# A four-way selective scan: another assignment of states to engines, and other costs for the planner that orders the scan pass

## Chip, cores and metric

The kernel runs on one core of one Trainium2 chip. The metric is the device time of one execution in microseconds, as the median of several runs. The core has five engines with instruction queues of their own: TensorE (PE; its weight loads are listed apart as PEld), VectorE (DVE), ScalarE (ACT), GpSimd (POOL) and SyncE (SP), which here only issues transfers.

## What is computed

Eight images of 64 x 64 positions with 96 channels go through a state-space layer and then through attention and a feed-forward layer. Nearly all of the time is in the selective scan of the first layer: 192 inner channels, 4 directions, 16 states, 4096 positions.

```
def _selective_scan(u, delta, A, Bs, Cs, D):
    def step(h, inps):
        d_t, u_t, b_t, c_t = inps
        h = h * jnp.exp(d_t[..., None] * A) + (d_t * u_t)[..., None] * b_t[:, :, None, :]
        y = jnp.einsum('bkdn,bkn->bkd', h, c_t)
        return (h, y)
    h0 = jnp.zeros(u.shape[:3] + (A.shape[-1],), u.dtype)
    _, ys = jax.lax.scan(step, h0, (dT, uT, BT, CT))
    y = jnp.moveaxis(ys, 0, -1)
    return y + D[None, :, :, None] * u
```

For each channel and each state n: a decay exp(delta·A), an input delta·u·B, a recurrence over the positions, and a sum over the states weighted by C. Group norm, projections, a 3 x 3 convolution and SiLU come before it; layer norm, gating, linear attention (no softmax) and a quantized feed-forward layer after it.

## The kernel before

`pass1` makes the scan's inputs, `pass2` is the scan, `pass3` the rest. Only `pass2` is concerned here.

**Chunks.** `pass2` works in 192 chunks (`pieces`, line 544) of 128 partitions by T = 1024 positions. A pair of images gives three kinds, c = 0, 1, 2. Kinds 0 and 1 hold the first 128 channels of one image each. Kind 2 holds the last 64 channels of both images ("two-batch chunk", `chunk_rows`, line 68). Each kind has 4 directions k with 4 chunks each, so it takes 16 chunks in a row. There are 128 chunks of kinds 0 and 1, and 64 of kind 2; the pass is a sequence of twelve sections of 16 chunks.

**One state of one chunk.** ACT makes the decay `da` (`decay`). The input times B, `dbu`, is made in PSUM, in a tile `wide`, in one of three ways, which `WAYS` (line 55) assigns by state, one pair of lists for kinds 0 and 1 and one for kind 2:

- by ACT (first list, `scaled`, line 651): ACT multiplies the transposed input `duT` by a column of B, in eight instructions of 128 x 128, or sixteen of 128 x 64 in a two-batch chunk, into a tile `x`; PE transposes it back into `wide` in eight instructions;
- by POOL (second list, `scaled_by_pool`, line 666): the same in one instruction of 128 x 1024, or two of 128 x 512, into `xg`; PE transposes it as before;
- by DVE (all other states, `products`, lines 691 to 699): PE spreads B over the partitions with two matmuls into `wide`, and DVE multiplies by `du`.

Then DVE runs the recurrence, `scan`, one TENSOR_TENSOR_SCAN per state. For each two states POOL multiplies by C (`times_c`, TENSOR_TENSOR c<-c,h) and PE adds the terms in `acc` (`sum_over_n`).

**Preparation.** While a chunk runs, `prepare` (line 561) makes the inputs of the next. It takes three `wide` tiles as well: for B transposed (PE wide<-sel,xb; ACT copies it to `bT`), for delta (PE wide<-xdt,dt_w; ACT computes the softplus, between two loads of its function tables) and for the transposed input (PE wide<-ident,du; ACT copies it to `duT`). POOL makes `du` from delta in between.

**Buffers.** Tiles come from rings (`room`, line 538): 3 `wide`, 3 `x`, 3 `da`, 3 `h`, 6 `c`, one `xg`. The n-th `wide` tile in the order of taking uses the buffer of the (n-3)-th, so whoever fills it first on PE waits until that one was read for the last time: by its scan on DVE, or by ACT's copy where it was a tile of the preparation.

**Order.** The order of the instructions on each engine is fixed when the program is built. Each step is a generator that yields the engine that it needs and a cost in us; `weave` (line 142) keeps a clock for each engine and always takes the step that can begin first, with a rank for ties, so the costs decide what stands ahead of what. `InOrder` (line 83) keeps every engine to that order. On the chip an engine works its queue in order: an instruction that has to wait holds up what stands behind it.

Of the kernel before, what the change touches and what calls it, by code (L numbers as in the profile page):

```python
# [51 lines left out]
NPC = L // T  # L52
NT = T // P

WAYS = [([2, 4, 6, 8, 10, 12, 14, 15], [3, 9]), ([3, 5, 7, 10, 13, 15], [2, 6, 12])]
NS = 3

LATE = 5
# [9 lines left out]
def chunk_rows(pair, c):  # L68

    b0 = 2 * pair  # L70
    if c < 2:
        return [(slice(0, P), b0 + c, slice(0, P))]
    return [(slice(64 * j, 64 * j + 64), b0 + j, slice(P, DI)) for j in range(2)]
# [456 lines left out]
def pass2(ctx, tc, g, ident, engines, fixed, u_d, xd_d, b_d, dt_d, y_d):  # L530
# [3 lines left out]
    pe, dve, act, pool = engines  # L534
# [4 lines left out]
    slots = {name: Slots(count) for name, count in room.items()}  # L539
# [9 lines left out]
    def take(name, shape, dtype=F32):  # L549

        return pools[name].tile(shape, dtype, name=name), slots[name].taken
# [6 lines left out]
    def spread(n, c):  # L558
        return sel[:, c, n : n + 1].to_broadcast([KB, P]) if c < 2 else sel2[:, n, :]
# [91 lines left out]
    def scaled(at, n):  # L651

        pair, c, _, _ = pieces[at]
        yield "duT", at
        x, (_, _, _, _, duT, bT) = None, made[at]
        for i in range(0, NT, 2):
            end = yield ("act", 0.6, 0.2) if i else ("act", 0.6, 0.2, slots["x"])
            if i == 0:
                x, slot = take("x", [P, NT, P])
            for i2 in (i, i + 1):  # L660
                for j, (part, _, _) in enumerate(chunk_rows(pair, c)):
                    act.mul(x[:, i2, part], duT[:, i2, part], bT[:, i2, j * N + n : j * N + n + 1])
        made["x", at, n] = x, "x", slot
        done["x", at, n] = end

    def scaled_by_pool(at, n):
        pair, c, _, _ = pieces[at]
        yield "duT", at
        end = yield "pool", 2.5, 0.2, slots["xg"]
        x, slot = take("xg", [P, NT, P])  # L670
        _, _, _, _, duT, bT = made[at]
        for j, (part, _, _) in enumerate(chunk_rows(pair, c)):
            wide = part.stop - part.start
            b = bT[:, :, j * N + n : j * N + n + 1].to_broadcast([P, NT, wide])
            pool.tensor_mul(x[:, :, part], duT[:, :, part], b)
        made["x", at, n] = x, "xg", slot
        done["x", at, n] = end

    def products(at, n):

        pair, c, _, _ = pieces[at]
        by_act, by_pool = WAYS[c // 2]
        if n in by_act or n in by_pool:
            yield "x", at, n
            end = yield "pe", 1.3, 0.2, slots["wide"]
            dbu, slot = take("wide", [P, T])
            x, name, of_x = made["x", at, n]
            for i in range(NT):
                pe.transpose(dbu[:, i * P : (i + 1) * P], x[:, i, :], ident)
            slots[name].release(of_x, end)  # L690
        else:
            yield "du", at
            end = yield "pe", 0.7, 0.2, slots["wide"]
            dbu, slot = take("wide", [P, T])
            xb = made[at][0]
            for q in range(0, T, GRP):
                pe.matmul(dbu[:, q : q + GRP], spread(n, c), xb[:, q : q + GRP], start=True, stop=True)
            end = yield "dve", 1.28, 0.0
            dve.tensor_mul(dbu, made[at][3], dbu)
        made["dbu", at, n] = dbu, slot  # L700
        done["dbu", at, n] = end
# [122 lines left out]
    for at, (pair, c, k, pc) in enumerate(pieces):  # L824
        by_act, by_pool = WAYS[c // 2]

        def add(kind, lead, unit, n=0):
            units.append((kind, at * N + n - lead, unit))

        add("prep", 8, prepare(at))  # L830
        for n in range(N):
            if n % 2 == 0:
                add("c", 12, load_c(at, n // 2), n)
            add("da", 2, decay(at, n), n)
            if n in by_act:
                add("x", 5, scaled(at, n), n)
            elif n in by_pool:
                add("xg", 4, scaled_by_pool(at, n), n)
            add("dbu", 1, products(at, n), n)
            add("scan", 0, scan(at, n), n)  # L840
            if n % 2 == 1:
                if at % NPC < NPC - 1:
                    add("carry", -2, carries(at, n // 2), n)
                add("term", 0, times_c(at, n // 2), n)
                add("sum", -4, sum_over_n(at, n // 2), n)
        add("acc", 0, take_acc(at), N)
# [289 lines left out]
```

## Time and profile before

| | |
|---|---|
| median of 3 runs | 10446.42 us (10441.61 to 10449.34) |
| the profiled execution | 10448.65 us, span 10446.9 us |
| scan pass, first to last recurrence | 758.9 to 9545.1 us of the span |
| one section of kinds 0 or 1 (16 chunks) | about 720 us |
| one section of kind 2 (16 chunks) | about 757 us |
| granted TensorE clock, mean | 0.896 |

A row of the costliest groups gives an engine, an operation, its result and operands with their shapes, the count, the busy time in us, the mean duration of one in ns, and the idle time of the engine just before. Busy time counts overlapping instructions once, so busy time divided by the count is less than the mean duration where instructions overlap. The table by windows gives for each stretch of time its length and then, for each engine, busy time and the number of instructions in brackets. The list of waits gives who waited for whom, the sum in us, how often, and the longest. In the timeline, equal instructions in a row are one line: start, length, engine, instruction, count, and in square brackets the idle time ahead of it and the releaser. All instructions carry line 91, a helper's line, and are told apart by the names of their tiles.

### The profile page before, as it was taken

To read this page: it belongs to the slowest core of one execution; us is meant where nothing else is said; L and a number is where in the kernel's file an instruction comes from. 1 tells how busy PE (TensorE), PEld (TensorE's weight loads), DVE (VectorE), ACT (ScalarE), POOL (GpSimd) and SP (SyncE) were. 2 spreads that over 40 slices of the span, in tenths; PEclk is the share of its full clock that TensorE was granted. 3 is DMA by queue.
4 is the path that set the end of the run, shared out by engine and by line. 5 is a ranking of instruction groups with operands and counts; after the bars stand their busy time and mean duration, and the time that the engine had idled before them with its cause. 6 is when DMAs were issued, how large, how long until landed. Compare 5 with 4: busy or idle time off the path is not lost.

```text
span 10446.9 us, 154273 instructions
## 1 busy us (share of the span) xinstructions
PE 7673.1 (73%) x52768; PEld 6378.4 (61%) x52768; DVE 9496.8 (91%) x6822; ACT 9405.8 (90%) x21523; POOL 9212.9 (88%) x3271
## 2 busy tenths in 40 slices
PE   6757777777777777777777777777777777776887
PEld 3326666666666666666666666666666666665775
DVE  6869999999999999999999999999999999997786
ACT  5759999999999999999999999999999999996665
POOL 1539999999999999999999999999999999997886
PEclk8879999998899999988999999989999999887776
DMA  5766676688976666788866666899666667897442
GB/s 153 234 189 218 220 237 211 220 206 198 206 216 211 214 221 201 219 201 198 220 213 214 217 209 215 203 200 209 219 206 218 217 203 220 200 199 181 128 131 61
DMA packets 928018, 2103.39 MB, mean 201 GB/s; under 512 B 274391, under 2 KB 422648, under 8 KB 925700
## 3 DMA queue, kind: packets, MB, share of 16 engines
q1 hardware_dynamic: 919812, 2092.79, 70.5%
q8 instruction: 422, 6.91, 0.3%
q14 instruction: 360, 2.95, 0.1%
q10 hardware_dynamic: 7424, 0.74, 0.1%
HBM read 1917.59 MB, written 175.66 MB: 200 GB/s over the span
## 4 chain that ended last, share of the span: by engine, by line
ACT 43%; DVE 17%; PE 15%; issue 14%; POOL 7%; DMA 4%; SPq 1%; ACTq 0%; DVEq 0%; POOLq 0%
ACT x L91 19%; ACT da L91 16%; DVE h L91 12%; PE acc L91 6%; PE wide L91 4%; POOL c L91 3%; DVE wide L91 3%; ACT L91 2%; PE mm L91 2%; ACT y L91 1%; ACT delta L91 1%; DMA xd_d<-xd 1%; ACT duT L91 1%; PE px L91 1%; PE pa L91 1%
## 5 line engine op out<-in xcount | busy, mean ns | idle before, releaser
L91 POOL TENSOR_TENSOR c<-c,h 128x2048 f32<-128x2048 f32 x1536 | 6964.2, 4551 | 260.9 <-DVE h L91 135.1
L91 DVE TENSOR_TENSOR_SCAN h<-da,carry,wide 128x1024 f32<-128x1024 f32 x2304 | 5262.1, 2331 | 283.0 <-PE wide L91 196.3
L91 ACT ACTIVATE x<-duT,bT 128x128 f32<-128x128 f32 (+1 forms) x14336 | 4188.5, 367 | 65.2 <-PE wide L91 60.9
L91 PE MATMUL acc<-ident,c 128*128 128x128 f32 x24576 | 3451.6, 296 | 653.8 <-POOL c L91 648.8
L91 PEld LDWEIGHTS acc<-ident,c 128*128 128x128 f32 x24576 | 3120.0, 154 | 982.8 <-POOL c L91 834.2
L91 ACT ACTIVATE da<-delta,a_neg 128x1024 f32<-128x1024 f32 x3072 | 3502.6, 1143 | 213.3 <-DVE h L91 201.6
L91 PE MATMUL wide<-ident,x 128*128 128x128 f32 x11264 | 1573.2, 287 | 661.1 <-DVE h L91 634.6
L91 PEld LDWEIGHTS wide<-ident,x 128*128 128x128 f32 x11264 | 1326.8, 147 | 926.3 <-issue 388.5
L91 DVE TENSOR_TENSOR_SCAN h<-da,wide 128x1024 f32<-128x1024 f32 x768 | 1709.6, 2271 | 114.7 <-PE wide L91 80.6
L91 DVE TENSOR_TENSOR wide<-du,wide 128x1024 f32<-128x1024 f32 x1216 | 1463.6, 1209 | 115.1 <-PE wide L91 115.0
L91 PE MATMUL wide<-xb,sel 96*128 96x512 bf16 x2432 | 760.8, 397 | 575.0 <-DVE h L91 470.1
L91 POOL TENSOR_TENSOR xg<-duT,bT 128x512 f32<-128x512 f32 (+1 forms) x640 | 892.0, 1409 | 107.7 <-PE wide L91 94.8
L91 PEld LDWEIGHTS <-sel 96*128 96x128 bf16 x2432 | 217.1, 100 | 725.3 <-DVE h L91 462.6
L91 POOL TENSOR_TENSOR du<-delta,u 128x1024 f32<-128x1024 f32 x192 | 455.0, 2370 | 200.2 <-ACT delta L91 91.1
L91 PE MATMUL wide<-ident,xg 128*128 128x128 f32 x3584 | 520.8, 293 | 131.0 <-DVE h L91 128.2
L91 PEld LDWEIGHTS wide<-ident,xg 128*128 128x128 f32 x3584 | 448.0, 153 | 175.3 <-issue 84.3
L91 ACT ACT_TABLE_LOAD x385 | 494.0, 1283 | 7.1
L91 DVE SCALAR_TENSOR_TENSOR u<-xpad,conv_w,u 128x4096 f32<-128x4096 f32 x96 | 456.2, 4752 | 1.9
L91 PE MATMUL px<-u,w_xp 128*128 128x512 f32 x512 | 256.8, 642 | 80.0 <-ACT u L91 47.9
L91 PE MATMUL wide<-ident,du 128*128 128x128 f32 x1536 | 213.8, 284 | 106.3 <-DVE h L91 77.9
L91 PE MATMUL mm<-w_out,gt 128*128 128x96 f32 (+1 forms) x1024 | 260.6, 374 | 34.6 <-POOL gt L91 16.4
L91 PEld LDWEIGHTS wide<-ident,du 128*128 128x128 f32 x1536 | 176.3, 146 | 137.7 <-issue 86.4
(133 smaller groups left out, 6271.4 us busy)
## 6 DMA issues: line engine op xcount, KB each, us to landing
c<-xd_d SPq DMA_DIRECT2D x1024, 1024.0 KB
c<-xd_d SPq DMA_DIRECT2D x1024, 512.0 KB
u<-u_d SPq DMA_DIRECT2D x128, 512.0 KB
xdt<-dt_d SPq DMA_DIRECT2D x1152, 36.0 KB
xb<-b_d SPq DMA_DIRECT2D x384, 96.0 KB
u<-u_d SPq DMA_DIRECT2D x128, 256.0 KB
y_d<-y SPq DMA_DIRECT2D x24, 1024.0 KB
y<-y_d SPq DMA_DIRECT2D x64, 384.0 KB
```

The source lines that it names most:

```text
L91: ins = getattr(self.engine, op)(*args, **kwargs).ins
```

## The change

Two things change, both inside `pass2`. The lists of states in `WAYS` are others. In kinds 0 and 1 the number of states for each engine stays at 8 for ACT, 2 for POOL and 6 for DVE. In kind 2 it goes from 6, 3 and 7 to 5, 3 and 8. And three of the costs that the planner reckons with are others: a quarter of an ACT product in a two-batch chunk 1.0 instead of 0.6 us, a POOL product 2.0 us (2.2 in a two-batch chunk) instead of 2.5 us, and a DVE product 1.22 instead of 1.28 us. The costs are used only when the program is built.

```diff
-WAYS = [([2, 4, 6, 8, 10, 12, 14, 15], [3, 9]), ([3, 5, 7, 10, 13, 15], [2, 6, 12])]
+WAYS = [([2, 5, 6, 8, 11, 12, 14, 15], [3, 7]), ([2, 3, 7, 9, 14], [0, 5, 12])]
...
         for i in range(0, NT, 2):
-            end = yield ("act", 0.6, 0.2) if i else ("act", 0.6, 0.2, slots["x"])
+            cost = 0.6 if c < 2 else 1.0
+            end = yield ("act", cost, 0.2) if i else ("act", cost, 0.2, slots["x"])
...
         yield "duT", at
-        end = yield "pool", 2.5, 0.2, slots["xg"]
+        end = yield "pool", 2.0 if c < 2 else 2.2, 0.2, slots["xg"]
         x, slot = take("xg", [P, NT, P])
...
-            end = yield "dve", 1.28, 0.0
+            end = yield "dve", 1.22, 0.0
             dve.tensor_mul(dbu, made[at][3], dbu)
```

## The prediction

> **What bounds the kernel now.** The page's first lines show three engines near full.
>
> ```profile
> PE 7673.1 (73%) x52768; PEld 6378.4 (61%) x52768; DVE 9496.8 (91%) x6822; ACT 9405.8 (90%) x21523; POOL 9212.9 (88%) x3271
> ```
>
> The average mixes stages, so I read the table by windows next: one section of kind 1, one of kind 2, then the first two directions (four chunks each) of the former. After the length come PE, PEld, DVE, ACT, POOL, then clock, DMA share and GB/s.
>
> ```profile
> 3679.90:4400.10 720.20, 527.43 (x3969) 460.07 (x3969) 684.85 (x353) 684.53 (x1491) 676.52 (x178) 0.93 0.66 214
> 4400.10:5157.30 757.20, 552.22 (x3889) 474.02 (x3888) 706.65 (x370) 744.12 (x1982) 713.06 (x240) 0.89 0.91 204
> 3679.90:3855.30 175.40, 130.62 (x989) 112.96 (x988) 170.55 (x89) 168.92 (x360) 167.53 (x44) 0.94 0.68 222
> 3855.30:4038.10 182.80, 129.09 (x948) 111.55 (x949) 172.18 (x89) 174.26 (x382) 170.38 (x46) 0.92 0.63 208
> ```
>
> Kind 2 is bound by ACT: 744.1 of 757.2 us, idle 13.1; DVE idles 50.6. Kinds 0 and 1 have no full engine: DVE and ACT idle 35 of 720 us each. In the list of waits, DVE's idle time there has one cause:
>
> ```profile
> DVE h L91 <- PE wide L91: 27.0, 14, 3.8
> DVE wide L91 <- PE wide L91: 2.8, 3, 1.5
> ```
>
> Fourteen waits in 16 chunks: about once a chunk. One of them in the timelines, DVE first, then PE:
>
> ```profile
> 3918.35 4.58 DVE L91 TENSOR_TENSOR_SCAN h<-da,carry,wide 128x1024 f32<-128x1024 f32 x2
> 3924.90 2.35 DVE L91 TENSOR_TENSOR_SCAN h<-da,carry,wide 128x1024 f32<-128x1024 f32 x1 [1.97 <-PE wide L91]
> ```
>
> ```profile
> 3915.03 1.07 PE L91 MATMUL wide<-ident,x 128*128 128x128 f32 x8 [1.72 <-DVE h L91]
> 3915.93 1.91 PE L91 MATMUL acc<-ident,c 128*128 128x128 f32 x16
> 3917.68 0.35 PE L91 MATMUL wide<-sel,xb 96*128 96x16 bf16 x8
> 3919.58 1.09 PE L91 MATMUL acc<-ident,c 128*128 128x128 f32 x8 [1.55 <-POOL c L91]
> 3920.75 0.75 PE L91 MATMUL wide<-xdt,dt_w 108*128 108x512 bf16 x2
> 3921.29 1.92 PE L91 MATMUL acc<-ident,c 128*128 128x128 f32 x8
> ```
>
> The x product is state 8. Two preparation tiles follow, B (sel,xb) and delta (xdt,dt_w), then state 9. With three `wide` buffers state 9 reuses state 8's, and PE cannot begin it before scan 8 ends (3922.9). DVE has nothing between scans 8 and 9, so it stands for the transposes' time. In the built order B and delta stand like this, with no product between, in 164 of 192 chunks. Matched with DVE's timeline: in kinds 0 and 1 the 105 such chunks wait 1.95 us ahead of state 9 and take 45.22 us; the 23 where a product stands between wait 0.06 and take 44.12. In the table above three of the first direction's four chunks are of the second sort, none of the second direction's.
>
> **What the skill says.** PSUM — Partial Sum Buffer, "Engine vs sequencer instructions": matmuls start and complete in program order, and the other engines' queues are strict FIFO. The PE rows agree. Perfetto Trace Analysis, "Optimization Strategy": the same gap repeating on an engine that should be saturated can mean too little SBUF or PSUM for the next tile; the gap at state 9 is one. ScalarE: Activation LUTs, "What ACT_TABLE_LOAD costs": an ACTIVATE with a pointer operand takes some 280 + 0.833·N ns and overlaps the next by 93 ns; for N = 64, 333 less 93 is 240. The trace has 336 and, by busy time over count, 254; I use 254.
>
> **The change part by part.** The rows for the prices:
>
> ```profile
> L91 ACT ACTIVATE x<-duT,bT 128x64 f32<-128x64 f32 x6144 | 1558.5, 336 | 7.3 <-PE wide L91 5.0
> L91 DVE TENSOR_TENSOR wide<-du,wide 128x1024 f32<-128x1024 f32 x1216 | 1463.6, 1209 | 115.1 <-PE wide L91 115.0
> ```
>
> (a) One state of each of 64 two-batch chunks leaves ACT for DVE. ACT loses 64 x 16 x 1558.5/6144 = 260 us, 65 a section: 744 becomes 679. DVE gains 64 x 1463.6/1216 = 77 us, 19.2 a section: 706.6 becomes 725.8. PE loses 8 transposes a chunk (1573.2/11264 = 0.140 each) and gains two matmuls (760.8/2432 = 0.313): less by 0.5 us, which costs nothing, as PE has 205 idle us in the section. The bound passes from ACT to DVE, with POOL (713) close behind.
>
> (b) The states moved between lists in kinds 0 and 1, and POOL's 2, 6, 12 to 0, 5, 12, change no count. Durations are the same, so they act only through the order, (c).
>
> (c) The new costs add and remove nothing; they move instructions. In the changed kernel's built order B and delta are adjacent in 5 chunks instead of 164: state 9 or 8 now stands between them. So the wait at state 9 goes from 159 chunks. What is late next: delta now waits for scan 8 instead of 7, and the copy to `duT` stands one state closer to its need. ACT still reaches softplus just after decay 11, one state before the product that takes delta's buffer, as before (decay 10, state 11). Every transfer stays, on SP; POOL's xg of state 7 stands six scans ahead of use (state 9's stood ten), enough at 2.6 us each. DMA in kind 2 is busy 0.91 x 757 = 687 us; in a shorter section this hides still, though it would be the next limit.
>
> What is left idle I take from the trace: the first direction above, mostly in the new pattern, leaves DVE 4.85 us in four chunks, 19.4 a section. Kinds 0 and 1: the eight sections took 5762.6 us with DVE busy 5479.9; 5479.9 + 8 x 19.4 = 5635, less by 127. (The comparison by chunks gives 105 x 1.10 = 116.) Kind 2: 3023.6 us in four sections, DVE busy 2823.1; plus 77 and 4 x 19.4 makes 2978, less by 46. Sum: 173 off the profiled execution's 10448.65, or 10275; the median stands 2.2 below, so **10273 us**.
>
> The residual idle is the one term that no row shows for the new order. Low end: the limiting engine idles only ACT's 13.1 us of today's kind 2. Then 5479.9 + 8 x 13.1 and 2900.1 + 4 x 13.1 give 249 less, 10198. High end: the next paragraph.
>
> **Rivals.** *Half given back.* ACT (684.5) and POOL (676.5) are as loaded as DVE in kinds 0 and 1, and a queue in order passes on any lateness. Only half of 127 arrives, and kind 2, now with DVE at 726 and POOL at 713, stands still: 10446 - 64 = 10382. For it: 0.7 us waits at state 7 already show in the 23 chunks. Against it: ACT reaches 98% in kind 2 today with the same queues.
>
> *A late first state in two-batch chunks* (slower). State 0 now goes through POOL: du, duT's copy on ACT, xg (2.1 us), PE (1.1), then the scan. Decay 15 stands ahead of the copy and needs scan 12's buffer; from there 1.05 + 1.0 + 2.1 + 1.1 = 5.3 us stand against three scans and two multiplications, 9.3. If a c term (4.55) comes between, 0.6 is missing; a second one makes it 5.1 a chunk. That is 64 x 5.1 = 326 on top, and without the gain in kind 2 the sum is -127 + 326: 10645. It decides against the change from 2.7 us a chunk (173/64). Against it: one c term stands there in the order, and starts after scan 11.
>
> *DVE idles as before.* If the stall only changes place, 35 and 50 us a section stay and (a) adds 77: 10523. Against it: the 23 chunks.
>
> *Nothing moves.* Excluded by the built order.
>
> **Chances.** Forecast 0.65 (10190 to 10345), half given back 0.22 (10345 to 10430), the two slower cases together 0.09, no visible change 0.04. The range, 10190 to 10400, holds the first and most of the second. About 0.2% (21 us) is what a measurement here can tell from no change. Faster 0.87, same 0.04, slower 0.09.
>
> **What would show it.** Right: windows of kinds 0 and 1 near 704 us with DVE busy still 685; of kind 2 near 745 with DVE 726 and ACT 679; DVE's wait for PE wide near 10 us a section instead of 30. Wrong: sections of 720 with the same wait at another state, or waits of DVE for a PE wide that waits for POOL xg at state 0.

## The result

The changed kernel takes 10286.21 us (median of 4 runs, 10274.94 to 10288.48), the kernel before 10447.88 (4 runs): a ratio of 0.9843, 95% interval 0.9826 to 0.986, or 162 us less. The forecast was 10273. The profiled execution of the changed kernel took 10274.94 us with a span of 10273.2, its fastest run; its span is 173.7 shorter than before.

From the page of the changed kernel, busy time, share of the span and instructions of each engine:

```profile
PE 7658.3 (75%) x52384; PEld 6303.1 (61%) x52384; DVE 9587.1 (93%) x6886; ACT 9155.6 (89%) x20499; POOL 9206.3 (90%) x3271
```

ACT has lost 250 us and DVE has gained 90. The table by windows, the sections of kind 1 and kind 2 that answer to those shown of before:

```profile
3617.30:4318.60 701.30, 533.44 (x3974) 457.03 (x3973) 685.78 (x352) 677.33 (x1481) 676.16 (x178) 0.93 0.69 220
4318.60:5060.60 742.00, 541.62 (x3785) 458.12 (x3784) 726.54 (x386) 694.72 (x1740) 712.75 (x239) 0.90 0.93 208
```

Kind 1 went from 720.2 to 701.3 us with DVE as busy as before: what went is idle time, 35 us down to 15.5. Kind 2 went from 757.2 to 742.0, and its fullest engine is now DVE (726.5), no longer ACT (694.7). Who DVE waited for in that section of kind 1 (sum, times, longest):

```profile
DVE h L91 <- PE wide L91: 4.0, 3, 2.7
DVE wide L91 <- PE wide L91: 1.4, 2, 0.7
```

Before, it was 27.0 and 2.8. The same place of a chunk as in the prediction, in the timelines of the changed kernel, PE first, then DVE:

```profile
4032.19 0.35 PE L91 MATMUL wide<-sel,xb 96*128 96x16 bf16 x8
4032.93 0.59 PE L91 MATMUL wide<-xb,sel 96*128 96x512 bf16 x2 [0.39 <-DVE h L91]
4034.90 1.45 PE L91 MATMUL acc<-ident,c 128*128 128x128 f32 x8 [1.38 <-POOL c L91]
4036.14 1.06 PE L91 MATMUL wide<-xdt,dt_w 108*128 108x512 bf16 x2
4036.99 1.06 PE L91 MATMUL wide<-xb,sel 96*128 96x512 bf16 x2
```

```profile
4028.32 6.80 DVE L91 TENSOR_TENSOR_SCAN h<-da,carry,wide 128x1024 f32<-128x1024 f32 x3
4035.03 1.21 DVE L91 TENSOR_TENSOR wide<-du,wide 128x1024 f32<-128x1024 f32 x1
4036.34 2.35 DVE L91 TENSOR_TENSOR_SCAN h<-da,carry,wide 128x1024 f32<-128x1024 f32 x1
4038.61 1.21 DVE L91 TENSOR_TENSOR wide<-du,wide 128x1024 f32<-128x1024 f32 x1
```

Product 9 (wide<-xb,sel at 4032.93) now stands between B's tile (sel,xb) and delta's (xdt,dt_w). PE fills it while DVE still runs the three scans that end with state 8, delta's tile waits in its place, and product 10 is ready before scan 9 ends. DVE's rows have no bracket: it did not stop. The two groups that priced the moved state, kept apart by shape:

```profile
L91 ACT ACTIVATE x<-duT,bT 128x64 f32<-128x64 f32 x5120 | 1315.5, 335 | 1.8
L91 DVE TENSOR_TENSOR wide<-du,wide 128x1024 f32<-128x1024 f32 x1280 | 1544.2, 1208 | 56.6 <-PE wide L91 54.9 <-ACT x L91 1.4 <-issue 0.2
```

1558.5 - 1315.5 = 243 us less on ACT (260 expected) and 1544.2 - 1463.6 = 81 more on DVE (77 expected).

### The profile page after: what moved, and what is told of

Read it like the earlier page. It is cut to its first block, busy times and chain, and to the rows that moved or that the text cites. A ratio compares the mean times of both kernels' runs of the same rounds, so it can differ in the third digit from the quotient of the medians.

```text
span 10273.2 us, 152438 instructions
## 1 busy us (share of the span) xinstructions
PE 7658.3 (75%) x52384; PEld 6303.1 (61%) x52384; DVE 9587.1 (93%) x6886; ACT 9155.6 (89%) x20499; POOL 9206.3 (90%) x3271
## 4 chain that ended last, share of the span: by engine, by line
ACT 29%; DVE 28%; issue 15%; PE 14%; POOL 10%; DMA 4%; SPq 1%; DVEq 0%; ACTq 0%; POOLq 0%
DVE h L91 20%; ACT x L91 11%; ACT da L91 11%; POOL c L91 7%; PE acc L91 6%; DVE wide L91 5%; PE wide L91 3%; ACT L91 2%; PE mm L91 2%; ACT y L91 1%; DVE u L91 1%; ACT delta L91 1%; POOL xg L91 1%; DMA xd_d<-xd 1%; DMA c<-xd_d 1%
## 5 line engine op out<-in xcount | busy, mean ns | idle before, releaser
L91 ACT ACTIVATE x<-duT,bT 128x128 f32<-128x128 f32 (+1 forms) x13312 | 3969.7, 368 | 1.9
L91 PEld LDWEIGHTS wide<-ident,x 128*128 128x128 f32 x10752 | 1304.4, 150 | 851.0 <-ACT x L91 393.0
L91 DVE TENSOR_TENSOR wide<-du,wide 128x1024 f32<-128x1024 f32 x1280 | 1544.2, 1208 | 56.6 <-PE wide L91 54.9
L91 PE MATMUL wide<-xb,sel 96*128 96x512 bf16 x2560 | 818.8, 403 | 692.6 <-DVE h L91 685.1
L91 PE MATMUL wide<-ident,xg 128*128 128x128 f32 x3584 | 483.2, 279 | 114.4 <-DVE h L91 112.6
L91 PEld LDWEIGHTS wide<-ident,xg 128*128 128x128 f32 x3584 | 411.5, 144 | 145.3 <-issue 111.7
L91 ACT COPY y<-acc 128x1024 f32<-128x1024 f32 x192 | 192.5, 1002 | 87.1 <-PE acc L91 86.7
L91 PEld LDWEIGHTS mm<-w_out,gt 128*128 128x128 f32 (+1 forms) x1024 | 202.0, 243 | 101.0 <-issue 34.6
```

Source lines behind the costliest of these rows:

```text
L91: ins = getattr(self.engine, op)(*args, **kwargs).ins
```

## The experiments

Two questions were open. The first is whether the neighbourhood of B's and delta's tiles was the cause in kinds 0 and 1. The second is what the costs and the lists do apart. All runs below were compared with the kernel before on the same chip (there 10460 us). The row "before" of the table, and its waits and lines below, come from the first chip, where it took 10448. The table gives the mean length of a section, from the first recurrence of one to that of the next, over the eight sections of kinds 0 and 1 and the four of kind 2, and in how many of the 128 and 64 chunks the two tiles are adjacent in the built order (the preparation ahead of the first chunk is counted with kinds 0 and 1). Waits ahead of one state are summed over DVE's timeline, those of more than 0.3 us.

| run | lists | costs | adjacent, kinds 0 and 1 | section, us | adjacent, kind 2 | section, us | time of the kernel, ratio and interval |
|---|---|---|---|---|---|---|---|
| before | old | old | 105 | 720.3 | 59 | 755.9 | 1 |
| changed | new | new | 1 | 705.3 | 4 | 740.6 | 0.9843 (0.9826 to 0.986) |
| e1 | old | old, forced apart | 1 | 702.4 | 0 | 790.2 | 0.9988 (0.9982 to 0.9995) |
| e2 | new | new, forced together | all | 709.9 | all but one | 764.5 | 0.9947 (0.9933 to 0.9962) |
| e3 | old / new | new | 115 | 710.0 | 0 | 740.4 | 0.9854 (0.9839 to 0.9869) |
| e4 | old | new | 101 | 709.2 | 25 | 763.5 | 0.9942 (0.9927 to 0.9957) |
| e5 | new | old | 29 | 697.5 | 63 | 785.5 | 0.9942 (0.9927 to 0.9957) |
| e6 | old / 4 on ACT | DVE's / new, apart | 111 | 713.5 | 0 | 758.3 | 0.9964 (0.995 to 0.9978) |
| e7 | old | POOL's / new, apart | 94 | 710.8 | 0 | 764.4 | 0.996 (0.9945 to 0.9975) |
| e8 | old / by turns | new, apart | 1 | 700.7 | 0 | 790.6 | 0.9984 (0.9978 to 0.9991) |
| e9 | old | old, two xg buffers | 105 | 713.9 | 59 | 755.5 | 0.9942 (0.9928 to 0.9957) |
| e10 | new | old, apart | 1 | 699.8 | 0 | 784.7 | 0.9959 (0.9944 to 0.9973) |
| e11 | new | old / new | 29 | 698.3 | 3 | 747.9 | 0.9795 (0.978 to 0.9809) |
| e12 | new | new | 1 | 705.5 | 4 | 741.5 | 0.9826 (0.9809 to 0.9842) |

Where a cell has two parts, the first is for kinds 0 and 1. The last row is the changed kernel again, on another chip: its sections agree with the first measurement to 1 us. In e6 to e8, e10 and e11 the helper's line is 95 or 96.

**e1: the tiles apart.** `prepare` waits for product 9 of the running chunk before it takes delta's tile. Lists and costs stay, but the planner then moves other instructions too:

```diff
+        if at > 0:
+            yield "dbu", at - 1, 9
         yield "pe", 0.9, 0.2, slots["wide"]
         pd, slot = take("wide", [P, T])
```

> The kernel before with its own lists and costs, and one line more: the tile of delta is taken only after the product of state 9 of the running chunk. In the built order B's and delta's tiles then stand next to each other in 1 chunk instead of 164. Theory (the ring of three wide buffers is the cause): kinds 0 and 1 go from 720 to about 704 us a section (-116 to -127 in all); kind 2 stays bound by ACT (744 busy), so at most its 13 idle us a section move: 750 to 757. Sum -120 to -150, about 10310. Rival (the gain came from the other lists of states or from taking work off ACT): 10446, and DVE waits as long at another state.

Kinds 0 and 1 did what the theory says: 702.4. DVE's wait ahead of state 9 fell from 206 us over the 128 chunks to 14, and hardly came back elsewhere (71 us at all other states, 60 before). Its waits in that run's section of kind 1, where it was 27.0 before:

```profile
DVE h L91 <- PE wide L91: 4.5, 8, 1.3
```

Kind 2 did not; it lost 34 us a section, and the two cancel. That the total, 10447, is the number of the rival is this cancelling. In that run's section of kind 2, by the list of waits, then the same of the kernel before:

```profile
DVE h L91 <- PE wide L91: 62.9, 20, 6.0
PE acc L91 <- ACT y L91: 48.4, 10, 6.6
```

```profile
DVE h L91 <- PE wide L91: 17.4, 13, 4.3
PE acc L91 <- ACT y L91: 18.5, 10, 4.3
```

PE stands 48.4 us waiting for ACT to copy the one `acc` tile out (ACT y); before the change it was 18.5. So the theory holds for kinds 0 and 1, and something else rules kind 2.

**e2: the changed kernel with the tiles forced together.** In `prepare` and `products`:

```diff
         pd, slot = take("wide", [P, T])
+        done["taken", at] = 0.0
...
+        if n in (9, 10, 11) and at + 1 < len(pieces):
+            yield "taken", at + 1
```

> The changed kernel with its own lists and costs, but products 9, 10 and 11 may be taken only after delta's tile of the next chunk, so that B's and delta's tiles stand next to each other in all 192 chunks. Theory: DVE waits again ahead of the next state: about 1.0 us a chunk where that state is DVE's own product (kinds 0 and 1, as at state 9 of kind 2 before), 128 us, and 1.3 to 1.9 where it is ACT's (kind 2, now bound by DVE), 83 to 120 us. 10286 becomes 10430 to 10530. Rival (the lists made the gain): within 30 us of 10286.

The time came out at 10403, below the expected span. Kind 2 paid 24 us a section; DVE's waits ahead of state 9 there are 91 us in all four sections, 1.4 a chunk, as expected. Kinds 0 and 1 paid only 4.6 a section. DVE does wait ahead of state 9 again, and longer than expected (184 us over 128 chunks, where the changed kernel has 4). Two things in its timeline make up for most of that. The waits of more than 0.3 us at other states fell from 0.55 to 0.13 us a chunk (the first chunk left out). And DVE now runs products 0 and 1, and 9 and 10, in pairs ahead of their scans (249 pairs of products, 16 in the changed kernel): its idle time between a product and a scan behind it fell from 10.3 to 3.0 us a section. So e2 changed more than the neighbourhood. A wait of 1.4 us a chunk cost 0.3 here, so the length of a wait at one state is not what its removal brings.

**e3 and e4: the lists in one place only, and the costs only.** e3 is the changed kernel with the old first pair of lists, e4 the changed kernel with both old pairs.

> The new costs and the new lists for two-batch chunks, the old lists for kinds 0 and 1. B and delta are adjacent in 115 chunks of kinds 0 and 1 and in none of kind 2. Theory: kinds 0 and 1 stay at 720 us a section, kind 2 goes from 757 to about 741: -64 in all, about 10383. Rival (kinds 0 and 1 gain from the costs alone): 10290.

> The new costs with the old lists. B and delta are adjacent in 101 chunks of kinds 0 and 1 and in 25 of kind 2. Theory: kinds 0 and 1 stay near 720 us a section (-0 to -10 in all); kind 2 stays bound by ACT with 744 us busy and can win no more than its 13 idle us a section, likely half of them: 750. Sum -10 to -40, about 10420. Rival (better costs are what made the gain): 10300.

e3 settled at 10309 and not at 10383: kinds 0 and 1 went down by 10 us a section with the tiles still adjacent in 115 chunks, so the rival was nearer. In e4 kinds 0 and 1 went down by 11, but kind 2 went up, and the time, 10401, is nearer to the theory's 10420 than to the rival's 10300; of the theory, kind 2 at 750 was wrong. DVE's wait at state 9 in kinds 0 and 1 fell to 138 us in e3 and 113 in e4, from 206. The costs alone shorten it. In kind 2, e3 is as good as the changed kernel, and e4, with the right costs and the old lists, is worse than the kernel before.

**e5: the lists only.** The kernel before with the new `WAYS`.

> The new lists with the old costs. B and delta are adjacent in 29 chunks of kinds 0 and 1 and in 63 of kind 2. Theory (lists and costs act through the order): kinds 0 and 1 about 706 us a section instead of 720, as few chunks are adjacent; kind 2 about 765, as in the run with the joined tiles, for DVE is the bound there and waits at state 9 again. Sum about -115 + 35, 10370. Rival (the state taken off ACT is worth its time whatever the order): kind 2 at 742, sum 10275.

Kinds 0 and 1 are the best of all runs, 697.5. Kind 2 took 785.5, more than either theory said: a state less on ACT, and 30 us more a section. DVE waits there 86 us ahead of state 9 in the four sections, as the theory has it, and another 69 ahead of state 6.

**e6 and e7: one cost for kinds 0 and 1, another question for kind 2.** In e6 POOL's old 2.5 stays for kinds 0 and 1, and in kind 2 state 9 goes from ACT to DVE; in e7 DVE's old 1.28 stays for kinds 0 and 1, and kind 2 has its old lists. In both, kind 2 has its tiles apart as in e1.

```diff
 e6: WAYS = [(..., [3, 9]), ([2, 3, 7, 14], [0, 5, 12])]
 e7: WAYS = [(..., [3, 9]), ([3, 5, 7, 10, 13, 15], [2, 6, 12])]
```

> Two things in sections that are read apart. Kinds 0 and 1: old lists, of the costs only DVE's product is new (1.22); B and delta are adjacent in 111 chunks. If DVE's cost is what shortens the waits there, about 706 us a section; if POOL's is, 720. Kind 2: new costs, delta's tile behind product 9, and one state more moved from ACT to DVE (4 states on ACT, 3 on POOL, 9 on DVE). Theory (DVE is the bound of kind 2 after the change): DVE busy 726 + 19 = 745, section 741 + 19 = 760. Rival (POOL or the order is the bound): 741 to 748.

> Kinds 0 and 1: old lists, of the costs only POOL's product is new (2.0); B and delta are adjacent in 94 chunks. If POOL's cost is what shortens the waits there, about 706 us a section; if DVE's is, 720. Kind 2: old lists (six states on ACT), new costs, delta's tile behind product 9. If a planner that knows ACT's cost only needs the tiles apart, ACT's 744 busy us bound it and the section takes 750 to 757; rival (an ACT that is nearly full loses time in any order but the old one): 765 to 790, as in the two runs with the old lists so far.

Either cost alone does most of it in kinds 0 and 1 (713.5 and 710.8 against 709.2 for all the costs), so it is no single number. In kind 2, e6 confirms the bound. The section of kind 2:

```profile
4392.20:5151.50 759.30, 534.87 (x3690) 444.05 (x3690) 744.15 (x402) 636.22 (x1476) 713.30 (x240) 0.90 0.92 204
```

DVE's busy time rose by 17.6 over the changed kernel's and the section by 17.3; ACT, with 123 us idle, is no help. In e7 the right costs with six states on ACT give 764, better than e1's 790 with the wrong ones, but not the old order's 756.

**e8: five and six states on ACT by turns.** New costs, the tiles apart in all kinds as in e1, old lists for kinds 0 and 1, and in every second two-batch chunk state 4 on ACT too.

```diff
+EVEN = ([2, 3, 4, 7, 9, 14], [0, 5, 12])
+def ways(c, pc):
+    return EVEN if c == 2 and pc % 2 else WAYS[c // 2]
```

> A version that may beat both: old lists for kinds 0 and 1, new costs, delta's tile behind product 9, and in two-batch chunks five and six states on ACT by turns (state 4 goes to ACT in every second chunk). Kinds 0 and 1: 702 us a section, as in the first run. Kind 2: mean busy times ACT 712, DVE 716, POOL 713 a section. If the buffers carry the imbalance from chunk to chunk, 730; rival (each chunk pays for its own bound, 46.5 us with six and 46.3 with five on ACT): 742 or more. Sum 10446 - 144 - 104 = 10200, or 10250 for the rival.

Kinds 0 and 1 came as expected, kind 2 not at all: 790.6. In the 32 chunks with six states on ACT, DVE waits ahead of state 4, 204 us in all. The built order and the trace show why. In these 32 chunks B's tile of the next chunk stands ahead of product 4 on PE, in all other two-batch chunks ahead of product 9. In one of them, PE, then DVE:

```profile
4522.70 0.39 PE L96 MATMUL wide<-sel,xb 96*128 96x32 bf16 x8 [4.29 <-DMA xb<-b_d]
4522.93 1.95 PE L96 MATMUL wide<-ident,x 128*128 128x128 f32 x8
```

```profile
4524.99 2.35 DVE L96 TENSOR_TENSOR_SCAN h<-da,carry,wide 128x1024 f32<-128x1024 f32 x1 [5.06 <-PE wide L96]
```

The transfer that brings B (xb) has not landed when PE comes to the tile, and product 4 stands behind it. PE waits for this transfer 109 us in the four sections of kind 2, in the changed kernel 1.3. What makes up the rest stays open. So the balance of busy times was not put to the test.

**e9: the old order with a second xg buffer.** Every engine's queue is the same, instruction for instruction; only the memory differs.

```diff
-tc.tile_pool(name=f"p2{name}", bufs=count, ...)
+tc.tile_pool(name=f"p2{name}", bufs=2 if name == "xg" else count, ...)
```

> The kernel before, instruction for instruction in the same order on all engines, with a second buffer for xg. POOL then no longer waits for PE to empty the only one (14.8 us in the section of kind 1). Theory (the wait at state 9 is a forced part of 1.25 us, from the ring of wide, and a rest from POOL's lateness, which holds PE at the acc matmuls that stand ahead of delta's tile and product 9): the waits of 2.4 to 3.7 us go, those of 1.25 stay, state 9 waits 1.3 a chunk instead of 1.95, kinds 0 and 1 fall from 720 to about 710 us a section, near the 707 of the new costs with the old lists. Kind 2 stays at 757 (POOL waits there for xg's buffer 0.6 us in all). Sum -80. Rival (POOL's wait is slack): 10446.

The list of waits of POOL in the section of kind 1, kernel before, then that of DVE for e9:

```profile
POOL xg L91 <- PE wide L91: 14.8, 12, 2.2
```

```profile
DVE h L91 <- PE wide L91: 18.4, 13, 2.3
DVE wide L91 <- PE wide L91: 1.3, 2, 0.7
```

The kernel took 10398 us, 62 less than the kernel before beside it, where 80 were expected. In e9 POOL's wait for the xg buffer is gone, and DVE's falls from 27.0 to 18.4, its longest from 3.8 to 2.3. The section is 710.0 instead of 720.2; the mean, which includes the first two sections, is 713.9. State 9 waits 1.55 us a chunk in the 105 chunks, not 1.95 and not 1.3. So part of that wait was not the ring of `wide`. A chunk of the kernel before shows the path; POOL, PE and DVE:

```profile
4314.39 1.92 POOL L91 TENSOR_TENSOR xg<-duT,bT 128x1024 f32<-128x1024 f32 x1 [2.19 <-PE wide L91]
...
4329.90 1.26 PE L91 MATMUL acc<-ident,c 128*128 128x128 f32 x8 [2.36 <-POOL c L91]
...
4334.95 4.58 DVE L91 TENSOR_TENSOR_SCAN h<-da,carry,wide 128x1024 f32<-128x1024 f32 x2 [3.70 <-PE wide L91]
```

POOL stood with an xg product for whose buffer PE had not yet come, the c terms behind it were late, and PE waited for a c term ahead of delta's tile and of product 9.

**e10: new lists, old costs, tiles apart.**

> New lists, old costs, delta's tile behind product 9 in all chunks. Kind 2: if the two tiles are what cost it 785 us a section with these lists and old costs, 745; if the planner's wrong cost of ACT is what spoils the order, 775 or more. Kinds 0 and 1: 29 chunks fewer with the tiles adjacent than in the run with the lists only, 692 to 697 us a section.

Parting the tiles brought kind 2 nothing: 784.7 apart, 785.5 adjacent in e5. DVE's wait ahead of state 9 went (86 us in e5's four sections, none here), but the one ahead of state 6 grew from 69 us to 183. With the new costs the same lists take 740.6, so the old costs spoil the order. Which of the three does was not tried one at a time in kind 2. The traces point to ACT's, and it is the furthest off: 1.6 us too low for a state, where POOL's is some 0.4 too high and DVE's 0.07. One of the waits ahead of state 6 in the timelines, PE, DVE, then ACT:

```profile
4746.57 1.91 PE L95 MATMUL wide<-ident,xg 128*128 128x128 f32 x8
4752.29 3.45 PE L95 MATMUL acc<-y,ident 128*128 128x128 f32 x16 [3.81 <-ACT y L95]
4755.58 0.60 PE L95 MATMUL wide<-xb,sel 96*128 96x512 bf16 x2
```

```profile
4746.68 4.45 DVE L95 TENSOR_TENSOR_SCAN h<-da,wide 128x1024 f32<-128x1024 f32 x2
4756.21 1.23 DVE L95 TENSOR_TENSOR wide<-du,wide 128x1024 f32<-128x1024 f32 x1 [5.08 <-PE wide L95]
```

```profile
4743.34 3.92 ACT L95 ACTIVATE x<-duT,bT 128x64 f32<-128x64 f32 x16
...
4751.25 0.99 ACT L95 COPY y<-acc 128x1024 f32<-128x1024 f32 x1
```

One state's sixteen products take ACT 3.92 us; the old costs say 2.4. The planner reckoned with 2.4 when it placed ACT's copy of `acc` behind them, and on the chip the copy comes later than planned. PE waits 3.81 us for it with the next product behind, and DVE waits 5.08. In this section of kind 2 PE waits 46.3 us for that copy, in the changed kernel 4.2. In e5 it is 18.3, no more than in the kernel before (18.5), so the copy does not explain all that the old costs did there.

Kinds 0 and 1 came out at 699.8, not at 692 to 697. There was little to win: in e5 their adjacent chunks wait 8 us in all ahead of state 9, 0.3 each. Adjacent tiles alone do not make a long wait.

**e11 and e12: the old costs for kinds 0 and 1, the new ones for kind 2, beside the changed kernel again.**

```diff
-        end = yield "pool", 2.0 if c < 2 else 2.2, 0.2, slots["xg"]
+        end = yield "pool", 2.5 if c < 2 else 2.2, 0.2, slots["xg"]
...
-            end = yield "dve", 1.22, 0.0
+            end = yield "dve", 1.28 if c < 2 else 1.22, 0.0
```

> A version that may beat both: the new lists for all kinds, the old costs for kinds 0 and 1 (POOL 2.5, DVE 1.28), the new ones for kind 2. Kinds 0 and 1 as in the run with the lists only, 696 us a section (5580 in all instead of 5643 in the changed kernel), kind 2 as in the changed kernel, 741. Sum 10286 - 63 = 10223. Rival (the order of one kind upsets the next, or the 29 adjacent chunks cost more here): 10286.

> The changed kernel on the same chip as the runs above, to compare with: 0.984 of the kernel before, about 10290; kinds 0 and 1 at 703 us a section, kind 2 at 741.

e11 is the fastest version: 10246.4 us (10234.84 to 10250.35) beside 10282.25 (10265.68 to 10290.33) for the changed kernel on the same chip, 36 less, where 63 were expected. Kinds 0 and 1 gave what was expected, 698.3. In kind 2 the first section took 762 and the other three 742 to 744; why the first one did stays open.

## Why the prediction was right, and where it was not

- *The time.* The two sums were 5635 us for kinds 0 and 1 and 2978 for kind 2; the profiled execution has 5642 and 2962. That is 120 and 61 us less than before, where 127 and 46 were expected, and the rest of the kernel outside the scan pass, which the prediction left as it was, took 7.5 more. The sum comes to 174 instead of 173 because these errors cancel, which is luck; by the medians it is 162.
- *The moved state (a).* The price was nearly right on both engines (243 for 260, 81 for 77), and the bound passed to DVE. In the section shown ACT is busy 694.7 us, not 679; as it no longer bounds the section, that cost nothing. What was left out: the gain needs the costs. The same lists planned with the old costs make kind 2 slower (e5, e10: 785). In e10 that is ACT's copy of `acc` coming late; that ACT's cost is the cause is argued from this trace, not shown by a run of its own. The prediction had (c) act in kind 2 through the neighbourhood of B's and delta's tiles alone. That is a step that failed, although its sum came out: parted with the old costs, kind 2 takes 790 with the old lists (e1) and 785 with the new ones (e10). With the new lists and costs together the neighbourhood does matter in kind 2, at 24 us a section (e2).
- *The wait at state 9 (c).* In the kernel before it comes from the two adjacent tiles in kinds 0 and 1: e1 parts them, the wait goes from 206 to 14 us, and 720 becomes 702. But the 1.95 us were mis-sized as one cause. With the order unchanged, a second xg buffer takes 0.4 of them (e9), and the new costs leave 1.1 to 1.2 in each adjacent chunk (e4: 113 us over 101 chunks, e3: 138 over 115). The gains overlap: apart 18 us a section, costs alone 11, both 20 (e1, e4, e8, old lists).
- *The lists in kinds 0 and 1 (b).* They change no count and act through the order, as said: with the old costs 697.5 instead of 720.3 (e5), but with the tiles apart in both only 699.8 instead of 702.4 (e10, e1). With the new lists the new costs lose 8 of these us, which e11 gets back.
- *The residual idle time.* Taken as 19.4 us a section from the first direction of the section of kind 1. It measured 15.5 in both sections shown, but over all sections 19.0 in kinds 0 and 1 and 14.5 in kind 2. DVE's busy time came out as summed (2904 us in kind 2 for 2900), so kind 2's extra gain is this term. It stood on four chunks; that it fits kinds 0 and 1 so well is partly luck.
- *The rivals.* The late first state of two-batch chunks did not come: DVE waits for PE wide 4.6 us in that whole section, three times, and in no two-batch chunk more than 0.3 us ahead of state 0. The copy to `duT` moved back by two decays in most chunks of kinds 0 and 1, not by one state; POOL waits for it 1.2 us in the section of kind 1. Half given back did not come in sum, though a part of the wait did move, to product 10 (30 us over 128 chunks, from the timeline of the changed kernel). DVE idle as before was wrong by the windows.

## What to carry to other kernels

Where three engines are filled to 95% and queues keep their order, time is lost at places, not in sums: find which buffer of a ring a late instruction reuses, and what stands ahead of it on its engine. Costs in the planner that were off, one of them by 1.6 us a state, made the plan worse even after the engine in question had been relieved (785 us a section instead of 756, and 741 with better costs), so measure costs by shape before moving work. An even balance of busy times is no gain when the order that goes with it waits (e8). A repeated wait can have two causes at one place; change the order with the memory kept, and the memory with the order kept, before giving it to one.
